# Block transposes and a packed DRAM detour for the fourth layer's softmax weights

## The chip, the cores and the metric

The kernel runs on one core of one Trainium2 chip. The metric is the device time of one execution in microseconds (us). All data are float32. TensorE (PE in the profile) multiplies and writes to PSUM; VectorE (DVE), ScalarE (ACT) and GpSimd (POOL) work on SBUF, and the first two on PSUM as well; SyncE (SP) issues nearly all DMAs.

## What is computed

Four attention layers are applied in sequence to `x`, eight batches of 128 tokens by 256 features; each attends to `ctx_2048`, eight batches of 128 tokens by 256. The first has 16 heads of 16 features, a key mask and an MLP. The second is a resampler: its keys are the context and the tokens themselves. The third ("wide") has two cross attentions of 16 heads of 128 features, each with one learned extra key, and an MLP. The fourth, which the change touches, has a self attention under a mask, a cross attention under another and an MLP:

```
def attention(q, k, v, mask):
    scores = jnp.einsum('bhqd,bhkd->bhqk', q, k) / jnp.sqrt(jnp.float32(HD))
    scores = scores * mask - 10000.0 * (1.0 - mask)
    probs = jax.nn.softmax(scores, axis=-1)
    return jnp.einsum('bhqk,bhkd->bhqd', probs, v)
...
ln_out = layernorm(hidden_states, ln1_s, ln1_b)
q, k, v = jnp.split(ln_out @ w_qkv + b_qkv, 3, axis=-1)
x = hidden_states + merge_heads(attention(..., ltor_mask)) @ w_ao + b_ao
ln_out = layernorm(x, ln2_s, ln2_b)
q = ln_out @ w_q + b_q
k, v = jnp.split(encoder_states @ w_kv + b_kv, 2, axis=-1)
x = x + merge_heads(attention(..., cross_mask)) @ w_co + b_co
ln_out = layernorm(x, ln3_s, ln3_b)
return x + gelu(ln_out @ w1 + b1) @ w2 + b2
```

## The kernel before

**Threads.** The eight batches are four threads of two batches (line 515). Each goes through all four layers (`blocks`, line 1460). Thread 2 starts when thread 0 is through its first two layers, thread 3 when thread 1 is (and when thread 0 has finished its wide layer); so at any time threads stand at different layers and fill each other's waits. In thread 3 the fourth layer is worked batch by batch (`BY_BATCH`, line 64), in the others both batches together.

**The order of the work.** It is fixed when the program is built. `Plan` (lines 85 to 225) simulates the engines with a cost per instruction (`_weight`, line 265) and starts, on each engine that falls free, the asked operation with the smallest urgency. Urgencies are the constants `U` (by kind of work) and `LATE` (by thread and layer), lines 66 and 67. On the chip each engine then runs its instructions in that order. Buffers are `Slots`, handed out in the same simulation. Where TensorE would fall idle in the plan, `idle_work` (line 425) puts in products of the identity that compute nothing, to keep its clock up; the profile shows them as `mm<-ident` and `tl<-ident`. Nearly every instruction is recorded through one helper, so the profile gives all of them line 337, and groups are told apart by the names of their tiles.

**PSUM.** Eight banks: `sc` four, used only as one unit for scores; `mm` two for projections; `tl` two for transposes and small products.

**The fourth layer's attention** (`by_pairs`, line 1106). For each batch:

1. `item` takes the four `sc` banks; 16 products give the scores of 16 heads, queries on the partitions, four heads in each bank `r`.
2. `softmax`, once for each `r`, takes one of seven `t` buffers (shared with the wide layer): VectorE multiplies scores by the mask, GpSimd adds the mask's offset, VectorE takes the minimum over keys (the scores are negated), ScalarE makes four exponentials with their sums, VectorE inverts the sums, GpSimd multiplies by them.
3. `values`: for each `r`, TensorE transposes the four 128x128 squares into a `tl` bank (lines 1166 to 1171), and ScalarE or VectorE, whichever comes free first, copies them into the tile `pts` (`out_of`, line 1207). `pts` is one of two `pt4` tiles (`pt_small`), taken when the first softmax is done; the first two layers use the same two for their exponentials (line 1046). 16 products per pair of heads then weigh the values (`weighted`, line 1180), and VectorE adds the bias.

In the profile, `pt4` tiles go by the name `pt`, like the wide layer's.

**The wide layer's weights** go another way (`turned`, line 1384): VectorE transposes the 32x32 blocks of `t` in place, four DMAs of 64 KB write the four bands of partitions to a DRAM buffer `d` so that the blocks stand in transposed order, and one DMA of 256 KB reads it back into a `pt` tile. All of them go through SP's one queue, as weight loads do.

Of the kernel before, what the change touches and what calls it, by code (L numbers as in the profile page):

```python
# [14 lines left out]
AF = mybir.ActivationFunctionType  # L15
ALU = mybir.AluOpType
AX = mybir.AxisListType

P = 128
# [41 lines left out]

WARM = True
FRONTS, WIDES = 2, 3
FRONT_BY_BATCH, BY_BATCH = (0,), (3,)
AHEAD = [[(1, 0), (1, 1)], [], [], []]
U = {'take': 0.75, 'taken': -1.08, 'norm': 1.94, 'mask': 3.99, 'k': 2.16, 'q': -0.04, 'v': 3.01, 'by key': -0.05, 'softmax': 7.79, 'weights': 0.61, 'pairs': 0.21, 'out': 0.57, 'mlp norm': -0.61, 'mlp 1': 2.92, 'mlp 2': 3.24, 'wide norm': -0.65, 'wide k': 3.4, 'wide q': 2.37, 'wide v': 6.37, 'wide s': 4.05, 'wide': 0.83, 'ahead': 3.34, 'load': -0.56, 'turn': -0.58, 'early': 3.32}
LATE = [(4.97, -3.47, -1, 3.41, 0.38, -0.78, 2.63, 6.4, 3.14, 4.12, 2.25, 1.84, 0.96, 5.29, -1.24, 0.08, 1.89), (2.66, 9.19, 7.29, 1.89, 2.36, 5.53, 5.25, 7.29, 7.81, 14.2, 3.59, 9.93, 12.52, 6.5, 7.55, 4.84, 5.27), (4.81, 10.83, 3.61, -1, -0.06, 1.37, 3.1, 3.46, -1.48, 1.98, 1.46, -1, -6.17, 8.35, 14.37, 7.29, 0.32), (1.56, 2.87, 0.11, -0.08, 1.95, 2.2, 4.51, 5.14, 0.3, -5.62, -8.12, 9.19, -0.97, 2.26, 3.5700000000000003, 0.86, 0.98)]


class Event:  # L70
# [14 lines left out]
class Plan:  # L85
# [263 lines left out]
def op(eng, f, lat=None, table=None):  # L349
    return ((eng, 0, f, lat, table),)  # L350
# [8 lines left out]
def four_blocks(ctx: ExitStack, tc: tile.TileContext, a: dict, out: bass.AP):  # L359
# [31 lines left out]

    NT_, NHT, NXN, NAT, NPT, ND = 7, 4, 2, 2, 3, 8
    t_slots, hT_slots, xn_slots, at_slots = Slots(NT_), Slots(NHT), Slots(NXN), Slots(NAT)
    pt_small, pt_wide, tm_slots, d_slots = Slots(2), Slots(NPT), Slots(2), Slots(ND)
    kb_slots, v_slots = Slots(20), Slots(4)
    attn_slots, x1_slots = Slots(4), Slots(4)
    row_slots, bv_slots, w_slots = Slots(2), Slots(2), Slots(NWT)
# [163 lines left out]
    def loader(T):  # L561
# [4 lines left out]
        for name, shape, pieces in names[:2] + ahead + names[2:]:  # L566
# [46 lines left out]
    def asks(r):  # L613
        yield r
# [5 lines left out]
    def each(*rs):  # L620

        for e in [spawn(asks(r), U["take"]) for r in rs]:
            yield e
# [140 lines left out]
    def product(ops, take, urgency=None):  # L764
# [12 lines left out]
    def mlp(T, name, src, e, w, b, b1, func, table, adds, to):  # L777
        hT, hT_in = yield from normed(T, src, e, w, b, adds, U["mlp norm"] + T.late)
        there, row_in = T.ready, T.row_in
# [19 lines left out]

        yield spawn(first(), U["mlp 1"] + T.late)  # L800
        for i in range(2):
# [9 lines left out]

        yield spawn(second(), U["mlp 2"] + T.late)

# [292 lines left out]
    def by_pairs(T, ns, scale, mask, masks, q, k, v, v_in, vb, attnT):  # L1106

        late = T.late
        heads = [(c, e) for c in range(NC) for e in range(2)]

        def item(b):
            yield (sc, 4)
            s = four_banks()

            def products():
                for j, (c, e) in enumerate(heads):
                    for r in range(4):
                        part = slice(32 * r, 32 * r + 32)
                        nc.tensor.matmul(
                            s[:, r, j * P : (j + 1) * P], lhsT=q[part, e, c, b],  # L1120
                            rhs=k[part, 0, c, b, 0], start=True, stop=True,
                        )

            yield op("PE", products)
            mn = new(act, [P, 4, 4], "mn", bufs=4)
            sm = new(act, [P, 4, 4, 1], "sm", bufs=4)
            ts = [None] * 4
            soft = [spawn(softmax(s[:, r], b, r, mn, sm, ts), U["softmax"] + late) for r in range(4)]
            return soft, ts

        def softmax(s, b, r, mn, sm, ts):
            s = s.rearrange("p (h k) -> p h k", h=4)
            yield (t_slots, 1)
            t = ts[r] = new(act, [P, 516], "t", bufs=NT_)[:, :512].rearrange("p (h k) -> p h k", h=4)
            bm = b % masks

            def over_heads(i):
                return mask[:, i, bm, :].unsqueeze(1).to_broadcast([P, 4, P])
            yield op("DVE", lambda: nc.vector.tensor_tensor(t, s, over_heads(0), ALU.mult))
            plan.put(sc)  # L1140
            yield op("POOL", lambda: nc.gpsimd.tensor_tensor(t, t, over_heads(1), ALU.add))
            yield op("DVE", lambda: nc.vector.tensor_reduce(mn[:, r].unsqueeze(2), t, AX.X, ALU.min))

            def exps():
                for j in range(4):
                    nc.scalar.activation(
                        t[:, j, :], t[:, j, :], AF.Exp, bias=mn[:, r, j : j + 1], scale=-1.0,
                        accum_out=sm[:, r, j],
                    )
            yield op("ACT", exps, None, EXP)  # L1150
            yield op("DVE", lambda: nc.vector.reciprocal(sm[:, r], sm[:, r]))
            yield op("POOL", lambda: nc.gpsimd.tensor_tensor(
                t, t, sm[:, r].to_broadcast([P, 4, P]), ALU.mult))

        def values(b, soft, ts, turn, next_turn):
            yield turn
            pts, evs = None, []
            for r in range(4):
                yield soft[r]
                if r == 0:  # L1160
                    yield (pt_small, 1)
                    pts = new(act, [P, 4, 4, P], "pt4", bufs=2)
# [12 lines left out]
            for ev in evs + v_in:  # L1175
                yield ev
            yield (tl, 1)
            av = parts(bank("tl"), NC, P)

            def weighted():  # L1180
                for i, (c, e) in enumerate(heads):
                    for r in range(4):
                        nc.tensor.matmul(
                            av[32 * r : 32 * r + 32, c, :],
                            lhsT=v[:, 0, b, 4 * c + r, 16 * e : 16 * e + 32],
                            rhs=pts[:, r, i, :], start=(e == 0), stop=(e == 1),
                        )
            yield op("PE", weighted)
            plan.put(pt_small)
            yield op("DVE", lambda: nc.vector.tensor_tensor(  # L1190
                attnT[:, :, b], av, vb.unsqueeze(2).to_broadcast([P, NC, P]), ALU.add))
            plan.put(tl)

        turn = Event()
        plan.set(turn)
        done = []
        for b in range(T.nb):
            soft, ts = yield from item(b)
            nxt = Event()
            done.append(spawn(values(b, soft, ts, turn, nxt), U["pairs"] + late))  # L1200
            turn = nxt
        return done

# [391 lines left out]
```

## Time and profile before

| | |
|---|---|
| median of 3 runs | 1179.25 us (1177.1 to 1180.3) |
| the profiled execution's own time | 1179.34 us |
| its span in the profile | 1177.5 us |
| granted TensorE clock, mean | 0.994 |
| busy, PE / DVE / ACT / POOL | 1130.4 / 784.0 / 581.2 / 308.0 us |
| transposes of `t` on TensorE (`tl<-ident,t`) | 256, 38.6 us |
| evictions of them on ScalarE and VectorE (`pt<-tl`) | 34 and 30, 19.5 and 20.0 us |
| block transposes on VectorE (wide layer) | 64, 44.5 us |
| moved by DMA | 171.86 MB, 146 GB/s in the mean |

The span runs from the first to the last instruction of the program on the core, and the execution's own time is a little longer. Busy times of TensorE count overlapping products once. "Idle before" in a group is the time that the engine waited just ahead of those instructions, with what ended the wait. The timeline merges neighbouring instructions of one kind; its columns are start, length, engine, line, operation, tiles (out<-in), shape, count.

### The profile page before, as it was taken

How to read it: one execution, taken by the hardware profiler on the slowest of the kernel's cores; microseconds unless marked ns; L12 is line 12 of the kernel's file. 1: busy time of each engine (PE TensorE's matmuls, PEld its weight loads, DVE VectorE, ACT ScalarE, POOL GpSimd, SP SyncE). 2: the span in 40 equal slices, each digit the busy share in tenths (PEclk: the TensorE clock that was granted, in tenths of full speed). 3: DMA queues.
4: the chain of work that ended last, by engine and by line, in shares of the span. 5: the costliest groups of instructions: out<-in, count | busy, mean ns of one | idle time of the engine just before them, and what ended most of it. 6: DMA issues, size and time to landing. Idle time of an engine off the chain costs nothing.

```text
span 1177.5 us, 22741 instructions
## 1 busy us (share of the span) xinstructions
PE 1130.4 (96%) x8280; PEld 925.4 (79%) x8280; DVE 784.0 (67%) x2126; ACT 581.2 (49%) x1475; POOL 308.0 (26%) x390
## 2 busy tenths in 40 slices
PE   8999889999999999999999999999999999989998
PEld 7687778787887888788878887788888877867776
DVE  7876767754668476668577858156754687785763
ACT  3445554343343354637534753223333384489783
POOL 3121211011211012014501522001111285384661
PEclk9999999999999999999999999999999999999999
DMA  7453233565564575555344645557665525522302
GB/s 249 129 161 90 73 99 104 154 187 160 169 185 139 154 212 164 162 159 152 118 123 137 182 155 166 181 167 217 211 193 172 166 81 150 179 85 86 99 1 64
DMA packets 151216, 171.86 MB, mean 146 GB/s; under 512 B 12128, under 2 KB 106048, under 8 KB 151104
## 3 DMA queue, kind: packets, MB, share of 16 engines
q1 hardware_dynamic: 149728, 169.23, 47.6%
q8 instruction: 66, 1.08, 0.4%
q10 hardware_dynamic: 1376, 1.18, 0.3%
q14 instruction: 46, 0.38, 0.1%
HBM read 152.52 MB, written 17.84 MB: 145 GB/s over the span
## 4 chain that ended last, share of the span: by engine, by line
PE 74%; DVE 10%; DMA 7%; ACT 5%; issue 2%; POOL 1%; SPq 1%; DVEq 0%; ACTq 0%; POOLq 0%
PE mm L337 56%; PE tl L337 14%; PE sc L337 4%; DMA pt<-d 2%; DVE t L337 1%; DVE mp L337 1%; ACT t L337 1%; ACT L337 1%; DVE rz L337 1%; DVE tm L337 1%; POOL t L337 1%; ACT kb L337 1%; DMA d<-t 1%; ACT q L337 1%; SPq L337 1%
## 5 line engine op out<-in xcount | busy, mean ns | idle before, releaser
L337 PE MATMUL mm<-hT,w 128*128 128x256 f32 (+1 forms) x1360 | 291.6, 362 | 9.6 <-ACT q L337 4.2
L337 PEld LDWEIGHTS mm<-hT,w 128*128 128x128 f32 x1360 | 233.9, 191 | 49.3 <-ACT kb L337 5.7
L337 POOL TENSOR_TENSOR t<-t,sm 128x512 f32<-128x512 f32 x128 | 132.2, 1040 | 458.8 <-DVE sm L337 271.1
L337 PE MATMUL mm<-ctxT,w 128*128 128x256 f32 (+1 forms) x632 | 144.8, 374 | 4.8 <-ACT q L337 2.6
L337 PE MATMUL mm<-w,ctxT 128*128 128x512 f32 (+1 forms) x352 | 144.6, 540 | 2.2 <-ACT kb L337 1.0
L337 PEld LDWEIGHTS mm<-ctxT,w 128*128 128x128 f32 x632 | 113.4, 190 | 23.1 <-ACT q L337 3.3
L337 PE MATMUL mm<-w,at 128*128 128x256 f32 x512 | 121.5, 381 | 2.0 <-DVE at L337 0.9
L337 POOL TENSOR_TENSOR x<-x,row 128x512 f32<-128x512 f32 (+1 forms) x42 | 46.7, 1114 | 293.3 <-ACT xn L337 135.0
L337 DVE TENSOR_TENSOR x<-mm,x 128x256 f32<-128x256 f32 (+1 forms) x98 | 46.6, 476 | 109.1 <-PE mm L337 108.7
L337 PE MATMUL mm<-w,kb 128*128 128x256 f32 x512 | 116.3, 380 | 0.2 <-ACT kb L337 0.2
L337 PEld LDWEIGHTS mm<-w,at 128*128 128x128 f32 x512 | 94.8, 190 | 19.7 <-issue 3.3
L337 PEld LDWEIGHTS mm<-w,kb 128*128 128x128 f32 x512 | 95.8, 190 | 14.6 <-issue 1.2
L337 ACT ACTIVATE t<-t,mn 128x128 f32<-128x128 f32 x256 | 99.1, 391 | 11.1 <-DVE mn L337 10.9
L337 PEld LDWEIGHTS mm<-w,ctxT 128*128 128x128 f32 x352 | 63.6, 191 | 41.5 <-issue 32.8
L337 ACT ACT_TABLE_LOAD x61 | 78.3, 1283 | 17.3 <-PE sc L337 8.0
L337 ACT ACTIVATE at<-tl,cols 128x128 f32<-128x128 f32 x200 | 56.5, 370 | 58.1 <-PE tl L337 50.1
L337 POOL TENSOR_TENSOR t<-t,mask 128x512 f32<-128x512 f32 x64 | 80.1, 1274 | 18.8 <-DVE t L337 16.3
L337 ACT ACTIVATE t<-t 128x516 f32<-128x516 f32 x64 | 40.3, 633 | 86.6 <-DVE t L337 77.9
L337 ACT ACTIVATE kb<-mm,sb 128x256 f32<-128x256 f32 x79 | 35.5, 471 | 96.2 <-PE mm L337 93.4
L337 ACT ACTIVATE kb<-mm,cols 128x256 f32<-128x256 f32 (+1 forms) x152 | 56.6, 440 | 49.1 <-PE mm L337 48.8
L337 PEld LDWEIGHTS tl<-pt,vw 128*128 128x128 f32 x512 | 64.3, 191 | 13.4 <-PE mm L337 3.6
L337 PE MATMUL tl<-pt,vw 128*128 128x128 f32 x512 | 67.7, 277 | 5.5 <-DMA pt<-d 4.8
(126 smaller groups left out, 1736.1 us busy)
## 6 DMA issues: line engine op xcount, KB each, us to landing
w<-in_L_wk SPq DMA_DIRECT2D x32, 512.0 KB, 4.6
w<-in_L_wv SPq DMA_DIRECT2D x32, 512.0 KB, 4.7
w<-in_L_wq SPq DMA_DIRECT2D x32, 512.0 KB, 5.0
w<-in_L_wo SPq DMA_DIRECT2D x32, 512.0 KB, 4.2
d<-t SPq DMA_DIRECT2D x256, 64.0 KB, 2.4
pt<-d SPq DMA_DIRECT2D x64, 256.0 KB, 3.9
bv<-dv SPq DMA_DIRECT2D x32, 256.0 KB, 4.8
w<-in_L_mlp_w SPq DMA_DIRECT2D x16, 512.0 KB, 4.6
```

Of the source, the lines that this page charges most:

```text
L337: return f(*args, **kw)
```

## The change

In threads 0, 1 and 2 (`TURNED`), the softmaxes of the fourth layer write into one tile `of` of 128 x (4 blocks of keys x 4 `r` x 4 heads x 32), a `pt4` tile, taken before the scores' banks. There the weights of a head stand in four runs of 32 keys. All operations of the softmax work on this order. After the last multiplication VectorE transposes 32x32 blocks in place, once for each `r`. When all four are done, `by_key` takes one of two new DRAM buffers `d4`, writes it with four DMAs of 256 KB and reads it back into the same tile with one of 1024 KB. The weighted products read it from there. The transposes on TensorE, the `tl` banks for them, their evictions and the `t` buffers of the softmax fall away in these threads; thread 3 keeps the old way. `U` and `LATE` have new values throughout.

```diff
+TURNED = (0, 1, 2)
-U = {'take': 0.75, 'taken': -1.08, 'norm': 1.94, 'mask': 3.99, ...
-LATE = [(4.97, -3.47, -1, 3.41, ...
+U = {'take': 1.74, 'taken': -0.68, 'norm': 2.11, 'mask': 6.32, ...
+LATE = [(3.96, -8.87, -1.32, 1.98, ...
...
         def item(b):
+            of = None
+            if T.h in TURNED:
+                yield (pt_small, 1)
+                of = new(act, [P, 4, 4, 4, 32], "pt4", bufs=2)
             yield (sc, 4)
             s = four_banks()
...
+        def softmax(s, b, r, mn, sm, ts, of):
+            if of is not None:
+                s = s.rearrange("p (h j c) -> p h j c", h=4, c=32)
+                t, keys = of[:, :, r].rearrange("p j h c -> p h j c"), AX.XY
+            else:
...
+            yield op("POOL", lambda: nc.gpsimd.tensor_tensor(t, t, inv.to_broadcast(list(t.shape)), ALU.mult))
+            if of is not None:
+                yield op("DVE", lambda: nc.vector.transpose(of[:, :, r], of[:, :, r]))
+
+        def by_key(b, soft, of):
+            for e in soft:
+                yield e
+            yield (d4_slots, 1)
+            d = new(dram, [P, 4 * 512], "d4", bufs=2)
+            to = d.rearrange("(j r) (i x) -> r i j x", j=4, i=4)
+            flat = of.rearrange("p j r h c -> p j (r h c)")
+            ends = [spawn(load(to[:, i], flat[32 * i : 32 * i + 32], 256), U["turn"]) for i in range(4)]
+            for e in ends:
+                yield e
+            yield spawn(load(flat, d.rearrange("p (i x) -> p i x", i=4), 1024), U["turn"])
+            plan.put(d4_slots)
+
+        def values(b, soft, ts, of, turn, next_turn):
             yield turn
             pts, evs = None, []
-            for r in range(4):
+            if of is not None:
+                evs.append(spawn(by_key(b, soft, of), U["weights"] + late))
+                of_head = of.rearrange("p i r h c -> p r h i c")
+            for r in range(4) if of is None else ():
...
-                            rhs=pts[:, r, i, :], start=(e == 0), stop=(e == 1),
+                            rhs=of_head[:, r, i], start=(e == 0), stop=(e == 1),
```

More of the change, by code (lines that the diff above doesn't have):

```diff
@@ L63 @@
 FRONTS, WIDES = 2, 3
+TURNED = (0, 1, 2)
 FRONT_BY_BATCH, BY_BATCH = (0,), (3,)
 AHEAD = [[(1, 0), (1, 1)], [], [], []]
-U = {'take': 0.75, 'taken': -1.08, 'norm': 1.94, 'mask': 3.99, 'k': 2.16, 'q': -0.04, 'v': 3.01, 'by key': -0.05, 'softmax': 7.79, 'weights': 0.61, 'pairs': 0.21, 'out': 0.57, 'mlp norm': -0.61, 'mlp 1': 2.92, 'mlp 2': 3.24, 'wide norm': -0.65, 'wide k': 3.4, 'wide q': 2.37, 'wide v': 6.37, 'wide s': 4.05, 'wide': 0.83, 'ahead': 3.34, 'load': -0.56, 'turn': -0.58, 'early': 3.32}
-LATE = [(4.97, -3.47, -1, 3.41, 0.38, -0.78, 2.63, 6.4, 3.14, 4.12, 2.25, 1.84, 0.96, 5.29, -1.24, 0.08, 1.89), (2.66, 9.19, 7.29, 1.89, 2.36, 5.53, 5.25, 7.29, 7.81, 14.2, 3.59, 9.93, 12.52, 6.5, 7.55, 4.84, 5.27), (4.81, 10.83, 3.61, -1, -0.06, 1.37, 3.1, 3.46, -1.48, 1.98, 1.46, -1, -6.17, 8.35, 14.37, 7.29, 0.32), (1.56, 2.87, 0.11, -0.08, 1.95, 2.2, 4.51, 5.14, 0.3, -5.62, -8.12, 9.19, -0.97, 2.26, 3.5700000000000003, 0.86, 0.98)]
+U = {'take': 1.74, 'taken': -0.68, 'norm': 2.11, 'mask': 6.32, 'k': 2.9, 'q': -2.43, 'v': 3.02, 'by key': -0.1, 'softmax': 9.01, 'weights': -1.42, 'pairs': 1.13, 'out': -0.04, 'mlp norm': 0.85, 'mlp 1': 4.55, 'mlp 2': 3.99, 'wide norm': 0.44, 'wide k': 2.76, 'wide q': 1.84, 'wide v': 6.38, 'wide s': 3.81, 'wide': 1.07, 'ahead': 10.48, 'load': 0.11, 'turn': -1.85, 'early': 1.64}
+LATE = [(3.96, -8.87, -1.32, 1.98, 0.96, -0.4, 2.93, 6.29, 3.39, 5.48, 0.6, 7.4, 1.95, 5.45, -6.16, -0.62, 6.08), (1.9, 10.16, 7.89, 1.93, 0.46, 5.77, 10.33, 7.81, 14.23, 27.77, 13.76, 7.05, 22.31, 13.12, 8.99, 5.42, 1.3), (5.01, 9.73, 4.44, -1.98, -0.12, 1.15, 3.93, 5.08, -0.21, 7.22, 5.02, 1.11, -10.5, 9.48, 12.66, -2.57, 5.82), (-1.77, 2.51, 0.32, -6.84, 2.1, 2.62, -10.52, 2.56, 9.9, -3.28, -16.64, 14.6, 1.64, 13.71, 2.39, 1.58, -5.33)]
 class Event:
@@ L393, in four_blocks @@
     t_slots, hT_slots, xn_slots, at_slots = Slots(NT_), Slots(NHT), Slots(NXN), Slots(NAT)
-    pt_small, pt_wide, tm_slots, d_slots = Slots(2), Slots(NPT), Slots(2), Slots(ND)
+    pt_small, pt_wide, tm_slots, d_slots, d4_slots = Slots(2), Slots(NPT), Slots(2), Slots(ND), Slots(2)
     kb_slots, v_slots = Slots(20), Slots(4)
@@ L1127, in item @@
             ts = [None] * 4
[L1128 to L1134, printed above, removed]
+            soft = [spawn(softmax(s[:, r], b, r, mn, sm, ts, of), U["softmax"] + late) for r in range(4)]
+            return soft, ts, of
+        def softmax(s, b, r, mn, sm, ts, of):
[3 more added lines that the diff above has]
+            else:
+                s = s.rearrange("p (h k) -> p h k", h=4)
+                yield (t_slots, 1)
+                t = ts[r] = new(act, [P, 516], "t", bufs=NT_)[:, :512].rearrange("p (h k) -> p h k", h=4)
+                keys = AX.X
             bm = b % masks
             def over_heads(i):
-                return mask[:, i, bm, :].unsqueeze(1).to_broadcast([P, 4, P])
+                m = mask[:, i, bm, :]
+                if of is not None:
+                    m = m.rearrange("p (j c) -> p j c", c=32)
+                return m.unsqueeze(1).to_broadcast(list(t.shape))
             yield op("DVE", lambda: nc.vector.tensor_tensor(t, s, over_heads(0), ALU.mult))
@@ L1141, in softmax @@
             yield op("POOL", lambda: nc.gpsimd.tensor_tensor(t, t, over_heads(1), ALU.add))
-            yield op("DVE", lambda: nc.vector.tensor_reduce(mn[:, r].unsqueeze(2), t, AX.X, ALU.min))
+            yield op("DVE", lambda: nc.vector.tensor_reduce(mn[:, r].unsqueeze(2), t, keys, ALU.min))
             def exps():
@@ L1146, in exps @@
                     nc.scalar.activation(
-                        t[:, j, :], t[:, j, :], AF.Exp, bias=mn[:, r, j : j + 1], scale=-1.0,
+                        t[:, j], t[:, j], AF.Exp, bias=mn[:, r, j : j + 1], scale=-1.0,
                         accum_out=sm[:, r, j],
@@ L1151, in softmax @@
             yield op("DVE", lambda: nc.vector.reciprocal(sm[:, r], sm[:, r]))
-            yield op("POOL", lambda: nc.gpsimd.tensor_tensor(
-                t, t, sm[:, r].to_broadcast([P, 4, P]), ALU.mult))
-        def values(b, soft, ts, turn, next_turn):
+            inv = sm[:, r] if of is None else sm[:, r].unsqueeze(3)
+            yield op("POOL", lambda: nc.gpsimd.tensor_tensor(t, t, inv.to_broadcast(list(t.shape)), ALU.mult))
[14 more added lines that the diff above has]
+        def values(b, soft, ts, of, turn, next_turn):
             yield turn
             pts, evs = None, []
-            for r in range(4):
+            if of is not None:
+                evs.append(spawn(by_key(b, soft, of), U["weights"] + late))
+                of_head = of.rearrange("p i r h c -> p r h i c")
+            for r in range(4) if of is None else ():
                 yield soft[r]
@@ L1161, in values @@
                     yield (pt_small, 1)
-                    pts = new(act, [P, 4, 4, P], "pt4", bufs=2)
+                    pts = of_head = new(act, [P, 4, 4, P], "pt4", bufs=2)
                 yield (tl, 1)
@@ L1197, in by_pairs @@
         for b in range(T.nb):
-            soft, ts = yield from item(b)
+            soft, ts, of = yield from item(b)
             nxt = Event()
-            done.append(spawn(values(b, soft, ts, turn, nxt), U["pairs"] + late))
+            done.append(spawn(values(b, soft, ts, of, turn, nxt), U["pairs"] + late))
             turn = nxt
```

## The prediction

> **What bounds the kernel now.** First the page's table of engines and its chain. 96% of the span is covered by matrix products, and the chain of work that ended last lies on TensorE for 74% of the time:
>
> ```profile
> PE 1130.4 (96%) x8280; PEld 925.4 (79%) x8280; DVE 784.0 (67%) x2126; ACT 581.2 (49%) x1475; POOL 308.0 (26%) x390
> ...
> PE 74%; DVE 10%; DMA 7%; ACT 5%; issue 2%; POOL 1%; SPq 1%; DVEq 0%; ACTq 0%; POOLq 0%
> ```
>
> A mean hides stages, so next the busy time in stretches. I cut them where the score products of the fourth layer lie in the timeline: thread 0 has its two attentions from 543 to 713 us, threads 1 and 2 their first ones from 938 to 994, and after 1020 come the second ones of threads 1 and 2 and all of thread 3. Columns: stretch, length, then busy time of PE, weight loads, VectorE, ScalarE, GpSimd, granted clock, DMA share, GB/s.
>
> ```profile
> 540.00:720.00 180.00, 178.99 (x1376) 145.65 (x1374) 131.21 (x328) 98.47 (x258) 59.66 (x66) 1.00 0.48 144
> 720.00:760.00 40.00, 36.14 (x169) 28.87 (x169) 16.56 (x46) 14.77 (x37) 4.92 (x7) 0.96 0.60 177
> ...
> 940.00:1020.00 80.00, 78.06 (x593) 62.90 (x592) 63.78 (x153) 46.55 (x179) 45.32 (x47) 1.00 0.40 118
> 1020.00:1178.00 158.00, 140.70 (x1188) 117.84 (x1186) 102.79 (x310) 115.86 (x375) 84.36 (x87) 0.96 0.26 79
> ```
>
> Up to 1020 us TensorE is the bound: 1.0 us idle in 180, 1.9 in 80. The last 157.5 us are different: PE is idle 17 us, and of its 140.7 another 10.8 are warming products that compute nothing (`mm<-ident` 10.2, `tl<-ident` 0.6). There the bound is a chain over all engines.
>
> **What the change removes.** Sixteen transposes and four evictions in each of 12 batch-attentions (three threads, two attentions, two batches): 192 of 256 transposes and 48 of 64 evictions. The groups of instructions by form, in the three stretches (count | busy us, mean ns | idle before):
>
> ```profile
> L337 PE MATMUL tl<-ident,t 128*128 128x128 f32 x64 | 9.2, 274 | 0.1
> ...
> L337 PE MATMUL tl<-ident,t 128*128 128x128 f32 x64 | 9.3, 275 | 0.6 <-ACT pt L337 0.4 <-POOL t L337 0.2
> ...
> L337 PE MATMUL tl<-ident,t 128*128 128x128 f32 x128 | 20.1, 287 | 3.2 <-POOL t L337 2.2 <-DVE pt L337 1.0
> ```
>
> A transpose's 274 ns is latency; they overlap, and 64 occupy 9.2 us. (a) Thread 0: **-9.2 us**, on the bound. (b) First attentions of threads 1 and 2: **-9.3 us**, on the bound. Packed tightest, eight take 1.04 us, so the two together are 16.6 at least. (c) Second attentions of threads 1 and 2: half of 20.1, 10.0 us of PE, but in the stretch that has 27.6 us without useful products. I take **0**, ends -10 and 0. Sum of PE: -18.5, at most -28.5.
>
> **What it adds on VectorE and takes from ScalarE.** Rows of the whole run:
>
> ```profile
> L337 DVE STREAM_TRANSPOSE t<-t 128x512 f32<-128x512 f32 x64 | 44.5, 699 | 3.3 <-POOL t L337 2.9
> ...
> L337 DVE COPY pt<-tl 128x512 f32<-128x512 f32 x30 | 20.0, 678 | 2.3 <-PE tl L337 2.1
> ...
> L337 ACT COPY pt<-tl 128x512 f32<-128x512 f32 x34 | 19.5, 587 | 20.4 <-PE tl L337 20.3
> ```
>
> 48 block transposes at 0.699 us are +33.6 us of VectorE; of the 48 evictions about 22 go from it (-15) and 26 from ScalarE (-15). VectorE gains 19 us on 784, ScalarE loses 15. Before 1020 both lie beside a full TensorE: 0. In the tail it is 16 of each: VectorE about +6 with 55 us idle there, ScalarE about -5 of 115.9. I take 0, ends -5 and +6. The softmax's new blocked order of the weights I cost at 0: the GpSimd multiplication has 1032 to 1059 ns over 128 instructions, half of which work in the blocked order already (the wide layer's), and VectorE's subtraction in that order takes 680 ns beside 679 for the plain mask product. The weighted products will read runs of 32; the wide layer's, which do so now, have the same 277 ns as the fourth layer's (`tl<-pt,vw` and `tl<-pt,v`). The exponentials in runs of 32 are not in the trace; nearest row 391 ns each, I take no change, ends 0 and +0.1 us each, which would be 6 us of ScalarE in the tail.
>
> Here a rule of the Trainium skill speaks against the change. The trace: four squares cost PE 0.60 us and an evictor 0.6 to 0.68; the block transpose alone costs VectorE 0.70 and leaves the blocks in the wrong partitions. The page "VectorE: DVE Perf Modes", section "Rules for kernel authors", says to use TensorE for a 128x128 transpose where PSUM is acceptable as its destination, and its section "The three transpose paths" gives 390 ns on TensorE and 311 ns on VectorE for one bf16 square. By those figures 192 squares would be an estimated 75 us of TensorE. The rule weighs one transpose by itself, not which engine is full; I go by the rows.
>
> **What it adds in waiting.** Issues of the wide layer's detour (KB each, median us to landing), the nearest rows:
>
> ```profile
> d<-t SPq DMA_DIRECT2D x256, 64.0 KB, 2.4
> pt<-d SPq DMA_DIRECT2D x64, 256.0 KB, 3.9
> ```
>
> Per batch the change writes four times 256 KB and reads 1024 KB. The queue moved 169.23 MB in 47.6% of 1177.5 us, 302 GB/s when busy, so 1.05 MB is 3.5 us each way. Less their own bytes, the rows keep 2.2 us for a write and 3.0 for a read: 5.7 + 6.5. With the last block transpose (0.7), less the last transposes and eviction that go (1.2), a batch's weights come **12 us later**. Ends: 0.7+2.4+3.9-1.2 = 6 if size costs nothing, 0.7+4x2.4+4x3.9-1.2 = 25 if everything goes in series. For thread 0 and for (b) the wide products of the other threads cover it. For the end it counts by thread. The results leave at:
>
> ```profile
> 1097.99 0.39 SPq L337 DMA_DIRECT2D out<-x  x1
> ...
> 1148.82 0.39 SPq L337 DMA_DIRECT2D out<-x  x1
> ...
> 1171.38 3.81 SPq L337 DMA_DIRECT2D out<-x  x2
> ```
>
> By the order in which they start: thread 1, then thread 2, then thread 3's two batches (thread 0's left at 772). Thread 2 is 22.6 us ahead of the end and gets two detours, 24 us: 1.4 over, and its MLP moves into thread 3's last softmaxes. I take **+2**, ends 0 and 2x25-22.6 = +27.
>
> The 60 added issues (0.43 and 0.34 us each, 25 us of SP) stand in SP's one queue: a write that waits for the fourth softmax holds the weight loads behind it, and TensorE waits for those. The weight tile is now taken before the scores and held to the weighted product; there are two, shared with the first layers' attention, whose exponentials wait behind it (at 582 to 627 us, thread 2, beside thread 0). If the other threads' wide products did not cover that, thread 2 would be up to one detour, 12 us, later; PE is idle 1.0 us there, so the cover is full and I take 0; freed `t` buffers also 0 (VectorE waited 1.1 us for them in all). The new urgencies reorder everything; no row prices that. I bound it by one stall like that of 720 to 760: ends -7.7 (below) and +7.7, taken as 0.
>
> **Sum.** The profiled execution took 1179.34 us, its span 1177.5 and 1.8 around it; the median is 1179.25, so one base. 1179.3 - 9.2 - 9.3 + 2 = **1163 us**.
>
> **Rivals.** *All of it is banked*: (c) counts too and thread 2's detours hide: 1179.3 - 28.5 = 1151, with a better order to 1143. For it: thread 1 ends 73 us early, and PE is busy 18.6 and 19.6 us of the twenties from 1060 to 1100. Against: 17 us idle there.
>
> *Thread 2 becomes the end*: its detours cost up to +27 in place of +2: 1170 to 1188, middle 1178. For it: only 22.6 us of lead; ScalarE is 74% busy there. Against: thread 2 also gains from its share of (a) and (b) ahead of its last attention, which keeps the lead.
>
> *Slower by stalls of the queue* (the other side). The trace has one such place. In 720 to 760 SP issues twelve writes of the wide detour in a row, the reads come late, and TensorE waits, then runs at half clock for 7.6 us:
>
> ```profile
> 735.54 5.72 SPq L337 DMA_DIRECT2D d<-t  x12
> ...
> 752.15 1.16 PE L337 MATMUL tl<-pt,vw 128*128 128x128 f32 x8 [2.44 <-DMA pt<-d]
> ```
>
> Price: 3.9 us idle and half of 7.6, 7.7 us a stall. If each of the four turned attentions before 1020 (two of thread 0, one each of threads 1 and 2) brings one: +30.8 - 18.5 = +12, 1192. It decides from three stalls on (18.5 / 7.7 = 2.4). Against it: where thread 0's attentions lie, the DMA share is 0.48 and PE is idle 1.0 us in 180, though wide detours run there.
>
> That the freed time is not freed (the plan fills it with warming products) would show as 1179 only if the end hung on something else before 1020, and nothing there is idle long enough.
>
> **Chances.** Forecast, 1156 to 1170: 0.45. All banked, below 1156: 0.25. Thread 2 the end, 1170 to 1188: 0.14 (0.05 faster, 0.04 same, 0.05 slower). Stalls, 1183 to 1199: 0.16, slower. Bound for no change 0.3%, 3.5 us, about what a measurement can tell: faster 0.75, same 0.04, slower 0.21. The range from 1146 to 1188 leaves out about 0.05 below and 0.10 above.
>
> **What would show it.** Right: `tl<-ident,t` x64 with some 10 us; PE busy 20 to 30 us less; 112 block transposes of 0.70; thread 0's result before 765 us (now 772); the span's last 150 us with more idle or warming PE than now. Detour: writes of 256 KB landing in 3 to 6 us, the read in 5 to 8. Wrong: PE waiting for `pt<-d` or for weights more than the 3.9 us of now before 1020, `out<-x` of thread 2 beside thread 3's, a clock under 1.00 before 1020, or a read of over 15 us.

## The result: slower by 0.9%

| | before | changed |
|---|---|---|
| median | 1179.25 us (1176.64 to 1182.55, 9 runs) | 1189.76 us (1183.69 to 1196.56, 9 runs) |
| ratio, 95% interval | | 1.009 [1.0063, 1.0117] |
| span of the profiled execution | 1177.5 us | 1194.7 us |

The forecast was 1163 us and faster; the time lies 1.8 us above the upper end of its range, 1188. The profiled execution of the changed kernel is the slowest of its nine (1196.56, 6.8 over the median), so differences of spans are larger here than those of medians, by which every price below goes.

The page of the changed kernel, its engines and its chain:

```profile
PE 1125.0 (94%) x8136; PEld 920.7 (77%) x8136; DVE 807.1 (68%) x2157; ACT 568.2 (48%) x1439; POOL 306.3 (26%) x386
...
PE 62%; DVE 14%; DMA 12%; ACT 7%; SPq 3%; issue 2%; POOL 1%; ACTq 0%; DVEq 0%; POOLq 0%
```

TensorE has 144 products fewer and only 5.4 us less busy time, and the share of DMA in the chain has gone from 7 to 12%. The same stretches as in the prediction, in the changed kernel (columns as there):

```profile
540.00:720.00 180.00, 171.23 (x1238) 136.13 (x1237) 127.76 (x322) 90.17 (x231) 46.82 (x51) 0.99 0.65 194
720.00:760.00 40.00, 38.22 (x195) 31.66 (x195) 19.66 (x51) 18.44 (x43) 4.83 (x6) 1.00 0.66 201
...
940.00:1020.00 80.00, 75.50 (x407) 59.44 (x406) 58.29 (x148) 42.47 (x124) 28.70 (x32) 0.98 0.72 225
1020.00:1195.00 175.00, 150.94 (x1271) 128.50 (x1269) 109.49 (x324) 106.79 (x375) 85.98 (x90) 0.94 0.39 117
```

The stretches that were full have holes: 8.8 us idle of 180 (before 1.0) and 4.5 of 80 (1.9). What ends the idle time, from the waits of TensorE (us in total, times, longest):

```profile
PE tl L338 <- DMA pt<-d: 19.7, 12, 7.0
PE mm L338 <- DMA w<-in_L_wq: 6.5, 4, 2.4
```

Before, the first was 4.8 us and the second missing. By tiles, 11.9 of the 19.7 are waits for the *wide* layer's weights (`tl<-pt,vw`), which the change does not touch, and 7.9 for the fourth layer's own, 0.8 of them before 1020 us. So the transfers that come late are mostly other threads' loads and reads in the same queue. SP's own waits (same columns) say how long the detour holds that queue:

```profile
SPq L338 <- DVE pt L338: 50.4, 7, 25.9
...
SPq L338 <- DMA d<-pt: 22.0, 12, 4.4
```

For 50 us its next instruction was a write that waited for VectorE's block transpose, for 22 a read that waited for the writes. One such place, SP's timeline (start, length, ...) and then TensorE's:

```profile
549.32 2.88 SPq L338 DMA_DIRECT2D d<-pt  x4
556.70 0.34 SPq L338 DMA_DIRECT2D pt<-d  x1
565.02 2.85 SPq L338 DMA_DIRECT2D d<-pt  x4
567.92 1.72 SPq L338 DMA_DIRECT2D w<-in_L_mlp_w  x1
569.69 0.64 SPq L338 DMA_DIRECT2D w<-in_L_wq  x1
```

```profile
573.15 1.08 PE L338 MATMUL tl<-pt,v 128*32 128x128 f32 x32
576.64 3.50 PE L338 MATMUL mm<-hT,w 128*128 128x256 f32 x8 [2.41 <-DMA w<-in_L_wq]
```

The first batch's writes hold the read until 556.7; then the second batch's writes, already next in the queue, hold it until their block transpose is done at 565.0. Another thread's weights (`w<-in_L_wq`) stand behind them, are issued at 569.7, land at 576.5, and TensorE is idle 2.41 us. Then eight products take 3.50 us, as the granted clock is at half from 576.3 to 579.8. In all the clock is at half for some 41 us of this execution, 14 before. The page "DMA: Bandwidth & Descriptors" of the Trainium skill, section "Anatomy of one DMA — SWDGE (gpsimd) path", says that DMA engines don't wait on semaphores and the issuing sequencer does, ahead of dispatch. That section is on GpSimd's path; SP's rows here agree with it (the write issued at 565.0, the loads behind it after that), and show what it means where unlike transfers share one sequencer.

The tail has a hole too. Thread 2's last attention is among the last work now:

```profile
1128.34 8.40 PE L338 MATMUL mm<-ident 128*128 128x128 f32 x48
1143.76 1.93 PE L338 MATMUL tl<-pt,v 128*32 128x128 f32 x32 [7.02 <-DMA pt<-d]
```

SP's timeline has the last results (threads 2 and 3):

```profile
1181.02 10.94 SPq L338 DMA_DIRECT2D out<-x  x3
```

From 1118 to 1144 TensorE has almost nothing but score products and 48 + 22 warming ones, until thread 2's own read lands. Its result leaves at 1181.0, beside thread 3's at 1186.2 and 1191.6; before, it was 22.6 us ahead.

TensorE's time by what it does, summed from the traces (useful: busy with anything but products of the identity alone; the rest is idle or warming), in us:

| kernel | useful | rest to 500 | rest 500 to 1020 | rest after 1020 | span |
|---|---|---|---|---|---|
| before | 1107.6 | 36.2 | 8.1 | 25.6 | 1177.5 |
| changed | 1093.0 | 36.9 | 23.8 | 41.0 | 1194.7 |
| changed, no detour (e2) | 1084.2 | 36.3 | 15.6 | 36.2 | 1172.3 |
| searched order (e8) | 1085.3 | 36.6 | 13.2 | 33.7 | 1168.7 |

The transposes did leave: without the detour 23 us of useful time are gone. In the changed kernel 9 of these come back, probably as its clock is at half for 24 us more than in e2, and 32 us of idle and warming time are added to before's, half of it ahead of 1020 and half behind.

### The profile page after: what moved, and what is told of

It reads as the page before. It is cut to its first block, busy times and chain, and to the rows that moved or that the text cites. A ratio compares the mean times of both kernels' runs of the same rounds, so it can differ in the third digit from the quotient of the medians.

```text
span 1194.7 us, 22428 instructions
## 1 busy us (share of the span) xinstructions
PE 1125.0 (94%) x8136; PEld 920.7 (77%) x8136; DVE 807.1 (68%) x2157; ACT 568.2 (48%) x1439; POOL 306.3 (26%) x386
## 4 chain that ended last, share of the span: by engine, by line
PE 62%; DVE 14%; DMA 12%; ACT 7%; SPq 3%; issue 2%; POOL 1%; ACTq 0%; DVEq 0%; POOLq 0%
PE mm L338 46%; PE tl L338 11%; DMA pt<-d 5%; PE sc L338 4%; SPq L338 3%; DVE t L338 3%; DMA w<-in_L_wq 2%; ACT pt L338 2%; DVE sm L338 2%; ACT L338 1%; DVE pt L338 1%; ACT q L338 1%; DVE tm L338 1%; DVE q L338 1%; ACT kb L338 1%
## 5 line engine op out<-in xcount | busy, mean ns | idle before, releaser
L338 POOL TENSOR_TENSOR t<-t,sm 128x512 f32<-128x512 f32 x80 | 83.0, 1040 | 371.4 <-DVE sm L338 207.9
L338 PEld LDWEIGHTS mm<-ctxT,w 128*128 128x128 f32 x632 | 114.1, 191 | 22.6 <-issue 3.1
L338 PEld LDWEIGHTS mm<-w,at 128*128 128x128 f32 x512 | 95.4, 190 | 18.5 <-issue 3.3
L338 ACT ACTIVATE at<-tl,cols 128x128 f32<-128x128 f32 x180 | 51.1, 368 | 84.9 <-PE tl L338 71.6
L338 PEld LDWEIGHTS tl<-pt,vw 128*128 128x128 f32 x512 | 65.9, 194 | 24.8 <-issue 13.2
L338 ACT ACTIVATE kb<-mm,sb 128x256 f32<-128x256 f32 x71 | 32.2, 472 | 109.2 <-PE mm L338 102.3
L338 PE MATMUL tl<-pt,vw 128*128 128x128 f32 x512 | 69.6, 281 | 13.5 <-DMA pt<-d 11.9
L338 ACT ACTIVATE pt<-pt,mn 128x128 f32<-128x128 f32 x192 | 74.2, 388 | 6.9 <-DVE mn L338 6.7
L338 PEld LDWEIGHTS tl<-kb,kb 128*128 128x128 f32 x512 | 64.7, 194 | 11.9 <-issue 6.4
```

Source lines behind the costliest of these rows:

```text
L338: return f(*args, **kw)
```

## The experiments

Runs e1 to e4, e5 and e6, e7 to e10, e11 and e12, and e13 to e15 were timed together, each group beside the kernel before, which took 1179.3 to 1180.6 us. Except where it says so, an edit keeps the order of the work on the engines.

**e1: what transposes cost.** Before, with each of the 192 transposes issued twice:

```diff
                         nc.tensor.transpose(
                             pt[:, i, :], ts[r].rearrange("p h k -> p (h k)")[:, i * P : (i + 1) * P], ident
                         )
+                        if T.h < 3:
+                            tc.nc.tensor.transpose(
+                                pt[:, i, :], ts[r].rearrange("p h k -> p (h k)")[:, i * P : (i + 1) * P], ident
+                            )
```

> The kernel before, its order kept, with each of the 192 transposes of threads 0 to 2 issued twice (the second writes the same square again). If a transpose is worth its 0.15 us of TensorE wherever TensorE is the bound, this costs what the prediction took as saved: 9.2 + 9.3 = 18.5 us before 1020 us and between 0 and 10 in the tail, so 1198 to 1208. If TensorE had room for them (they fill gaps that are there anyway), under 8 us: below 1187.

1191.96 us, ratio 1.0113 [1.0081, 1.0144]: +12.4. The busy time of TensorE grew by 19.2 us, 0.10 for each where the prediction had 0.14. Matched product by product, the lag behind the kernel before grows by some 5 us in thread 0's stretch, by 6 from 923 to 1004 us, and by 3 in the tail (this execution is the slowest of its four, 16.9 us behind in all). So the gain to be had is real, but of the order of 12 us rather than 18.5, as far as adding measures what removing brings.

**e2 and e3: the detour taken out, or small.** The changed kernel without the ten transfers of an attention (e2), and with an eighth of their bytes (e3):

```diff
-            ends = [spawn(load(to[:, i], flat[32 * i : 32 * i + 32], 256), U["turn"]) for i in range(4)]
+            ends = [spawn(dma(unsent, 256, False), U["turn"]) for i in range(4)]
...
-            yield spawn(load(flat, d.rearrange("p (i x) -> p i x", i=4), 1024), U["turn"])
+            yield spawn(dma(unsent, 1024, False), U["turn"])
```

> The kernel after, its order and its plan kept, without the detour: the four writes and the read of each batch are not sent, so the fourth layer's weights in threads 0 to 2 stay transposed within blocks only, and SP issues 60 DMAs less. Theory 1, the detour is what costs (its landing comes later than the order allows for, in the tail of thread 2 and at some places before): it falls to 1150 to 1170, below before. Theory 2, the new order of everything is slower on the chip whatever the detour does: it stays above 1180.

> The kernel after, its order kept, with the detour's DMAs moving an eighth of their bytes (64 of 512 columns per block, so most of the fourth layer's weights of threads 0 to 2 stay in the wrong place). Fixed latency and waits on the queue stay, time on the wire goes. If the bytes are the cost (read 7.1 us instead of some 3, other loads slowed), it comes down most of the way that the kernel without the detour does; if the fixed latency and the dependence are, it stays within 5 us of after, 1185 to 1190.

1173.01 us (0.995 [0.9932, 0.9968]) and 1172.80 us (0.995 [0.993, 0.997]). The detour costs the changed kernel 17 us; without it the change gains 6.6 us, less than theory 1 of e2 had (1150 to 1170). With an eighth of the bytes the whole price goes too, but e3 took away more than bytes, and its expectation ("waits on the queue stay") was wrong. The 64 columns that are left belong to `r` = 0, so a write waits for the first of the four block transposes, not the last: in the place above, the second batch's writes go out at 549.0, not 565.0. SP's waits for VectorE's block transposes before 1020 us, in the changed kernel and then in e3:

```profile
SPq L338 <- DVE pt L338: 17.3, 4, 7.9
SPq L338 <- DVE pt L338: 0.6, 2, 0.3
```

So e3 doesn't tell the size of the transfers from their wait.

**e4 and e6: the urgencies and the number of threads.** The changed code with `U` and `LATE` of before (e4), and with `TURNED = (0, 1)` (e6); both give another order.

> The kernel after with the U and LATE of before: the new way of the weights alone, planned with the old urgencies. Theory 2 (the new urgencies are the loss): 1160 to 1175. Theory 1 (the detour is the loss): 1185 to 1215, since nothing has been moved to make room for it and thread 2's weights come late in the tail.

> The kernel after with thread 2 worked in the old way (TURNED = (0, 1)), planned anew with the urgencies of after, so the order changes too. Theory 1b with the tail: a third of the detour's bytes and thread 2's waits in the tail go, a third of the transposes come back (+4 by the doubled transposes): some 6 + 6 - 4 less, 1178 to 1185. If the turned thread 2 was no part of the loss: 1190 or more.

1221.83 us (1.0362 [1.0341, 1.0382]) and 1188.35 us (1.0077 [1.0049, 1.0104]). The change can't be had without new urgencies. Sparing thread 2 its detours doesn't help by itself, with urgencies that were made for three turned threads.

**e5: the bytes alone.** The four writes are sent from a tile that is long there, and a copy from DRAM to DRAM takes the place of the read. The copy still waits for its writes on SP (33.0 us in all), but VectorE is not waited for, and TensorE waits for nothing of it.

```diff
+            apart = ctxT.rearrange("p c (j x) -> p (c j) x", x=512)
-            ends = [spawn(load(to[:, i], flat[32 * i : 32 * i + 32], 256), U["turn"]) for i in range(4)]
+            ends = [spawn(load(to[:, i], apart[32 * i : 32 * i + 32], 256), U["turn"]) for i in range(4)]
...
-            yield spawn(load(flat, d.rearrange("p (i x) -> p i x", i=4), 1024), U["turn"])
+            d2 = new(dram, [P, 4 * 512], "d5", bufs=2)
+            yield spawn(load(d2, d, 1024), U["turn"])
```

> The kernel after, its order kept, with all of the detour's bytes on the wire but nothing waiting for them: the four writes of each batch take their 256 KB from the context tile, the read goes from that DRAM buffer to another one, so the fourth layer's weights in threads 0 to 2 stay transposed within blocks only. Theory 1a, the loss is that the weights come late to their own products: it falls to the 1173 of the kernel without the detour. Theory 1b, the loss is that other transfers (the wide layers' weights and detours) come late behind these bytes: of the 17 us between after and the kernel without the detour the 14 that arose before 1020 us stay, 1183 to 1188, and only the tail's 6 go.

1177.87 us (0.9984 [0.9967, 1.0002]): 4.9 of the 17 us are bytes in the way of other bytes. Neither theory was right alone: the other 12 come with the dependence, at full size. Whether small transfers with the same waits would cost them too, no run shows.

**e13 and e14: which dependence.** e13 takes only the second half of e5's edit (real writes, the copy in place of the read), e14 only the first (early writes, the real read).

> The changed kernel, its order kept, with the detour's read replaced by a copy of the same bytes from DRAM to DRAM, which waits for the writes as the read does, but nobody waits for it: the writes still wait for VectorE's last block transpose, the products take the weights without their exchange between partitions (so the fourth layer's values of three threads are other ones). Against the run with the bytes alone (1177.9) it adds the writes' wait. Theory A1 (SP's queue, held by writes that wait for VectorE, is what costs): 1184 to 1190. Theory A2 (TensorE's wait for the weights that land late is what costs): 1175 to 1180.

> The changed kernel, its order kept, with the detour's writes sent from another tile that is long there, so that they don't wait for VectorE, and the real read, for which the products wait (it brings other values, so the fourth layer's outputs of three threads are other ones). The read still waits for the last block transpose, but no more for writes behind it, so the weights land some 7 us (the writes' 6.5 to 9 us) sooner after it. Theory A1: 1176 to 1181, as SP is held less. Theory A2: between 1178 and 1188, as TensorE still waits for a read, a shorter time. Both below 1182 here, with e13 at 1184 or more, says A1; e13 below 1180 and this one above 1183 says A2; both in the middle says that the two add.

e13 1185.05 us (1.0036 [1.0009, 1.0062]), e14 1177.69 us (0.9986 [0.9965, 1.0007]). SP's waits in e13:

```profile
SPq L338 <- DVE pt L338: 47.8, 7, 25.2
SPq L338 <- DMA d<-pt: 22.1, 15, 4.4
```

and in e14, where both rows are the read's, which waits for its writes to land and for VectorE, the writes being already sent:

```profile
SPq L338 <- DMA d<-ctxT: 26.2, 14, 7.2
SPq L338 <- DVE pt L338: 24.5, 5, 16.9
```

In e13 nobody reads what the detour brings, and still it costs 7.2 us more than e5: the writes that wait for VectorE at the head of SP's queue. In e14 TensorE waits for a real read, but one that is not late, and it costs nothing more than e5. So the 17 us are, in steps of the runs (the intervals of neighbours touch at most): bytes 4.9 (e2 to e5), writes that hold the queue 7.2 (e5 to e13), TensorE's waits for what then lands late 4.7 (e13 to the changed kernel). By the ratios to the kernel before, which moved by up to 1.4 us between the groups, they are 4.0, 6.1 and 6.4.

The hold costs where loads stand behind it. Before 1020 us SP waits 15.7 us for VectorE's block transposes in e13, 0.8 in e14 and not at all in e5; matched instruction by instruction on VectorE, e13 is 9.0 us behind e5 at 1020. After that SP waits another 32.1 us in e13, at most 25.2 at a time, and e13 falls no further behind: 7.6 us at the end.

**e7 and e15: another queue.** The detour issued by GpSimd (e7) or by ScalarE (e15) at the same places:

```diff
-            ends = [spawn(load(to[:, i], flat[32 * i : 32 * i + 32], 256), U["turn"]) for i in range(4)]
+            ends = [spawn(dma(lambda _, i=i: nc.gpsimd.dma_start(out=to[:, i], in_=flat[32 * i : 32 * i + 32]), 256, False), U["turn"]) for i in range(4)]
```

> The changed kernel with the ten-transfer detours (four writes and the read of each batch) issued from POOL's DMA queue in place of SP's, each at the place in time where the order had it; the order of PE, VectorE and ScalarE is the same, instruction for instruction. Theory A: most of the detour's 17 us (1189.8 against 1173.0 without it) is SP's one queue: a write that waits for VectorE's last block transpose holds the wide layers' loads behind it. Then with another queue those loads go out on time, and what remains is the bytes (1177.9 where full bytes move and nothing waits) and the weights' own landing in the tail: 1177 to 1183. Theory B: what costs is that the fourth layer's weights themselves land late, whatever queue they go by: 1186 to 1193, and PE's waits for weights stay. Theory C: POOL, which also multiplies the softmax by its inverse sums in order, is held by the same wait and gives back what SP saves: over 1193, with DVE waiting for POOL more than before.

> The changed kernel with the detour's transfers issued from ScalarE's DMA queue in place of SP's, each at its place in time; the order of PE, VectorE and POOL is kept. It puts the wait for the writes' landing on ScalarE, which copies TensorE's results out of PSUM and takes the softmax's exponentials in order. Theory A1: the wide layers' loads go out on time, but ScalarE is held about 7 us for each of the 12 reads, and TensorE waits for its copies: over 1195, and PE's waits for DMA w<-in_L_wq are gone while those for ACT grow by more than 10 us. Rival: ScalarE has slack enough at these places (568 us busy of 1195), and it is 1175 to 1186.

1203.74 us (1.0201 [1.0136, 1.0266]) and 1198.28 us (1.0148 [1.0104, 1.0192]): slower than by SP (for e15 in the median; its interval overlaps with the changed kernel's). The waits of GpSimd in e7 have a new row, and the first of TensorE's has grown (shown in this order):

```profile
POOL pt L338 <- DMA d<-pt: 35.6, 8, 8.3
```

```profile
PE tl L338 <- DMA pt<-d: 31.5, 13, 11.2
```

TensorE's wait for `w<-in_L_wq` is 1.2 us in e7 and 1.0 us in e15, so those loads do go out on time, as theory A said. But GpSimd multiplies the weights by their inverse sums in order, and is held 35.6 us for the writes' landing, ahead of the read; the next batch's weights come later still. The hold moves to whatever issues the transfers. For e15 the rows are less plain: TensorE's waits for ScalarE are 4 us longer for `pt` and little else, not the 10 us that were expected. But the profile puts a hold of ScalarE by a transfer down to other engines, and the timelines show it, first ScalarE's and then TensorE's:

```profile
564.72 0.37 ACT L338 COPY v<-mm 128x256 f32<-128x256 f32 x1 [10.34 <-PE tl L338]
572.40 1.88 ACT L338 ACTIVATE pt<-sc 128x2048 f32<-128x2048 f32 x1 [4.14 <-issue]
```

```profile
574.33 1.13 PE L338 MATMUL tl<-pt,v 128*32 128x128 f32 x32 [3.99 <-ACT pt L338]
```

In the first gap ScalarE stands at a write until VectorE's block transpose ends at 561.3, and then issues four of them; in the second it stands at the read, issued at 572.0, until the last of them has landed, at 571.9. SP isn't free of the detour either: 31.8 us of its waits in e15 are put down to the landing of `d<-pt`. What each of these is worth I leave open.

**e8, e9, e10: an order made for the real transfers.** The kernel's planner counts a DMA as 2.75 us per 1024 KB and 2.3 more, 5.1 for the detour's read, which takes 7.1 on the chip. These three have 3.4 and 2.6 there, and urgencies searched anew in the planner, in the same way, for three, no and two turned threads:

```diff
-        plan.dma_until = max(plan.dma_until, plan.now) + kb_ * 2.75
-        yield plan.dma_until - plan.now + 2300
+        plan.dma_until = max(plan.dma_until, plan.now) + kb_ * 3.4
+        yield plan.dma_until - plan.now + 2600
```

> The changed kernel with its planner told that a DMA takes 3.4 us per 1024 KB and 2.6 us on top (it has 2.75 and 2.3; the profile of the changed kernel has 7.1 us for a read of 1024 KB under load, the planner 5.1), and with urgencies searched anew under that. The planner's own end is then 1155.6 us, against 1196.3 for the changed kernel's urgencies under the same costs. Theory A (the detour's price is one of placing: transfers that land later than the order allowed for hold SP's queue and PE): an order that allows for them loses little to the detour, so 1162 to 1175, below the kernel before. Theory B (the price stays wherever the detour is placed, as the bytes and the waits of the weights are the same): 1180 to 1192. It is read beside the two other searched orders of this call, made in the same way.

> The control of the searched orders: the kernel before, no thread's weights turned by the detour, its planner given the same slower transfers and its urgencies searched anew for the same time. The planner's end is 1170.4 us, 14.8 above that of the searched kernel with three threads turned. Theory A: the chip follows the planner once transfers have their real cost, so this one is 10 to 18 us above the searched three: 1174 to 1188. Theory B: what the search brings is the search's alone and the turned threads add cost: this one is below the searched three by 5 or more.

> The same search with threads 0 and 1 turned and thread 2 left with TensorE's transposes, so that no detour lies in the last 100 us. The planner's end is 1159.7 us, 4.1 above the searched three. Theory A: 1164 to 1178, beside or a little above the searched three. If the detour of thread 2, near the end, is what can't be hidden (its own read was 7.0 us of PE's waits in the tail of the changed kernel), this one is below the searched three by 3 to 8 us although the planner says otherwise.

e8 **1172.33 us**, ratio 0.9937 [0.9912, 0.9961]; e9 1190.62 (1.0083 [1.0052, 1.0113]); e10 1185.37 (1.0042 [1.0017, 1.0067]). With the same work and the same detour, e8 is 17.4 us below the changed kernel and below the one before, and in e9 the same search without the detour gives a slower kernel, not a faster one. e9 and e10 both came out slower than expected (1174 to 1188 and 1164 to 1178): the planner has e10 4.1 us above e8, the chip 13.0. So the new costs don't make a good order by themselves, and no run separates them from the search in e8. Its page:

```profile
PE   9999988999989999999999999999999999978898
...
PEclk9999999999999999999999999999999999999999
```

These are the busy tenths of TensorE and its granted clock in 40 slices; the clock is full all through. TensorE's and then SP's waits in e8:

```profile
PE tl L338 <- DMA pt<-d: 5.8, 5, 2.9
```

```profile
SPq L338 <- DVE pt L338: 46.0, 8, 9.4
SPq L338 <- DMA d<-pt: 9.2, 4, 4.0
```

SP waits for VectorE nearly as long as in the changed kernel (46 us), but at most 9.4 at a time, not 25.9. One of its places in SP's timeline:

```profile
618.73 2.98 SPq L338 DMA_DIRECT2D d<-pt  x4
621.80 5.12 SPq L338 DMA_DIRECT2D d<-t  x8
626.97 0.45 SPq L338 DMA_DIRECT2D w<-in_L_wk  x1
627.47 2.34 SPq L338 DMA_DIRECT2D pt<-d  x2
```

Between the writes and the read stand eight writes and a load of others, so SP works while the detour's writes land. And thread 2's result leaves at 1139.3, 21.6 us ahead of thread 3's first.

**e11 and e12: what is the order's, what the detour's.** e8 with an eighth of the bytes (the edit of e3, which takes away waits as well), and the changed kernel with `TURNED = ()`, that is, new urgencies with the old transposes.

> The searched kernel with three threads turned (1172.3 us), its order kept instruction for instruction, with the detour's transfers cut to an eighth of their bytes (the rest of the weights is not exchanged between partitions, so the fourth layer's values of three threads are other ones). The same cut took 17 us off the changed kernel (1189.8 to 1172.8). Theory A (the price of the detour was one of placing): the searched order leaves little of it to take away, so 1167 to 1172. Theory B (the detour always costs about as much, and the searched order is better for other reasons): 1153 to 1160.

> The changed kernel with its list of turned threads empty: the fourth layer's weights of every thread go by TensorE's transposes again, and only the new urgencies stay; the planner's end is 1169 us, 16 above the kernel before and 27 above the changed kernel. Theory: the urgencies were fitted to a planner in which the turned weights cost TensorE nothing, so without them the order is worse than the old one: 1185 to 1205, that is, above the kernel before, which says that the new order is no gain by itself and the 6.6 us of the changed kernel without its detour (1173.0) are what the saved transposes leave. Rival: the new urgencies are a better order in themselves, and this kernel is at or below 1179; then the saved transposes bring still less than 6.6 us on the chip.

1165.93 us (0.9885 [0.9869, 0.9902]) and 1202.62 us (1.0195 [1.0152, 1.0238]). The same cut that took 17 us off the changed kernel takes 6.4 off e8, so some 10 us of the price were its placing, and theory A's 1167 to 1172 was a little too high. The new urgencies are no better order in themselves.

## Why the prediction was wrong, point by point

- **(a) and (b), -18.5 on the bound: right in sign, too large.** The transposes were a price on the bound (e1: 12.4 us for all 192), and the rows before predicted what would go: 64 remaining transposes with 10.6 us, 112 block transposes of 0.69 to 0.70 us, a little less of ScalarE and 23 us more of VectorE. But TensorE gave up more than that, 23 us in e2, and the end came only 6.6 us sooner: e2 has 7.5 us more rest from 500 to 1020, and 10.6 more in the tail. "The cover is full" was read from before, and the transposes were part of the cover; but e2 has the new order too, and no run separates the two. Two signs of being right failed: PE's busy time fell by 5.4 us, not 20 to 30, and thread 0's result left at 802.8, not before 765.
- **(c) 0: nearly right.** The doubled transposes added 3 us in the tail.
- **The detour's durations: right.** Writes 4.6 us (predicted 3 to 6), read 7.1 (5 to 8). From the last block transpose to the landing of the read the 12 batches take 11.3 to 17.8 us, 14.4 in the mean; the prediction's sum was 12.2. The fourth layer's products do wait for them little before 1020 (0.8 us), as predicted.
- **"I take 0" for SP's one queue: the step that failed.** The prediction saw that "a write that waits for the fourth softmax holds the weight loads behind it, and TensorE waits for those", and dismissed it as PE's cover was full. But a full TensorE of before is no cover against its own loads coming late: those are its work. The runs put 17 us on the detour, 12 of them from the hold and what lands late by it, where the prediction had 0 for the queue and 2 for thread 2's end. Of the 27 us between the forecast and the measured time, some 15 lie here and some 12 in the gain above.
- **The new urgencies, taken as 0 between -7.7 and +7.7.** Their size was underestimated both ways: the same work spans 1172 (e8) to 1222 (e4) by the planned order alone.
- **Thread 2's lead of 22.6 us, +2 on the end.** The lead was a fact of the old order. The new one has thread 2 beside thread 3 even without the detour (results at 1158.7 and 1163.8 in e2), and the tail waits 7.0 us for its read. That the lead can be kept, e8 shows.
- **The rival "Slower by stalls of the queue"** had the right mechanism and 1192, near the time, but both its terms were too large: 30.8 for the stalls (17 measured), 18.5 for the gain (6.6). The price of one stall was misread: in the place from which it is taken, the granted clock is at half for 3.4 us (753.6 to 757.0; its own row has 0.96 of 40 us), not 7.6. That makes a stall 5.6 us and four of them 22.4, and the bound of 7.7 on the urgencies rests on the same figure. Of the four signs that were to say the forecast is wrong, three were seen: waits for DMA before 1020 (19 us for `pt<-d` and `w<-in_L_wq`), a clock under 1.00 there, and `out<-x` of thread 2 beside thread 3's; no read took over 15 us.
- **The rule on transposes** from "VectorE: DVE Perf Modes" was weighed against TensorE's full time. By e8 that choice can stand: with its order the turned kernel is 0.6% faster than before. What the change lost lay in neither engine's transposes.

What stays open: how much of the 6.4 us that the detour still costs in e8 is bytes and how much waits; whether the hold would cost as much with small transfers; and what each hold in e15 is worth.

## What to carry to other kernels

A new store to DRAM that waits for a late producer can cost what stands behind it in its queue (7.2 us here): list the loads issued after it, by whom they are awaited, and place something between the write and its read. An engine that is 99% busy hides latency of others' work, not of its own inputs. And where an order is made by a plan, one order doesn't measure a change: here the same work was 0.9% slower or 0.6% faster, and a plan with durations nearer to the measured ones gave both the fastest order (e8) and, for the kernel before, one slower than the old (e9).

## What the runs showed of the hardware

- An idle time of 2.41 us on TensorE was followed by 3.4 us at half clock (576.3 to 579.8 in the changed kernel). One of 2.94 us in e8, ahead of the products at 1044.1, was not: the clock of e8 is full all through. So in these runs the length of one gap doesn't decide it. The page "TensorE: Matmul & The Clock Gate", section "What's actually happening", has the clock fall after an idle window of about 3.4 us; both gaps here were shorter than that, and after one of them the clock fell.
- A second transpose issued right behind the same first one took 0.10 us of TensorE's busy time (19.2 us for 192), where in the kernel before the tightest eight took 0.13 each (1.04 us together).
- Reads of 1024 KB took 7.1 us in the median among other traffic, and 5.5 in e14, where the writes ahead of them went out earlier.
